# A 7x7 depthwise convolution as matmuls: the halo loads' queue and who empties PSUM

## The chip, the cores and the metric

The kernel runs on one core of one Trainium2 chip. The metric is the device time of one execution in microseconds. A core has five engines that run their own instruction streams: TensorE (PE in the profile, PEld for its weight loads), VectorE (DVE), ScalarE (ACT), GpSimd (POOL) and SyncE (SP). DMAs are issued from SP, ACT or POOL and are carried out by 16 DMA engines. Matmuls write into PSUM, from which DVE and ACT copy to SBUF.

## The reference

Two layers over a tensor x of 384 channels and 192 x 192 pixels, in fp32. Layer 0 is an attention over channels; layer 1 is a depthwise 7x7 convolution. Each takes a group norm of its input and adds its result to it:

```
x = x + L0_conv(groupnorm(x))       # qkv 1x1, 2x2 max pool, 3x3 depthwise, channel attention, gelu, repeat, projection
x = x + L1_conv(groupnorm(x))       # what the change touches

def L1_conv(x, weight):             # weight: (384, 1, 7, 7)
    w_sym = (weight + rot90(weight, 1) + rot90(weight, 2) + rot90(weight, 3)) * 0.25
    return depthwise_conv(x, w_sym, stride=1, pad=3)
```

## The kernel before

The kernel goes through the image four times. It reads x for the statistics of the first norm; computes pooled, depthwise-filtered q, k and v and the products of q and k; mixes v and writes the input of layer 1, channel by channel, into DRAM tiles `sd` and `sh` (L558 to L642); and last does the 7x7 stage (L651 to L853), which the change is in.

**The 7x7 stage** takes 8 channels (CB) in each of 48 steps. A channel's 192 rows are cut into 6 tiles (NT) of 32 rows (TR), and its columns into 4 classes by their remainder modulo 4 (CP). So 4 x 32 = 128 partitions hold one channel's rows by column class, and the free dimension is 6 tiles x 48 columns (NJ) = 288. The 7x7 filter becomes three matmuls per channel that add up in PSUM: two with `main`, the second one column along, and one with `aux`, which holds in partitions 0 to 63 a copy of a part of `main`, shifted by two columns, and in partitions 64 to 93 and 96 to 125 the halo: three rows above and three below each tile, in 10 column classes (NQ). The weight matrices, 128 x 384 per channel, were built earlier and lie in DRAM tile `wt`.

**The loop** (L809) is software-pipelined by hand. In iteration n it traces, in this order: the loads of step n + 2 (`load_w` L675: one DMA of 1536 KB; `load_main` L680: one of 1200 KB for `main`, two of 281.2 KB for the halo in `aux`); on POOL the `borders` of step n + 1 (L741: two corrections at the columns at the edges, the shifted copy into `aux` at L761, two corrections at its edges, and two fills at L770 where the halo lies outside the image); on POOL and SP the `spread` of step n - 1 (L790: two interleaving copies at L794 from `apart` to `res`, then eight stores of 144 KB at L798, the first four after the first copy, the others after the second); and then the matmuls of step n (L825, L830, L836) with their evictions. Between the second and the third pair of channels DVE adds the residual's diagonal to the next step's weights (`middle`, L784).

**Evictions.** A pair of channels, q of 0 to 3, has one PSUM tile `ps` of two banks; four such tiles are in rotation. Each is emptied in four pieces, one for each quarter g of 32 partitions, with both channels at once (32 x 576 elements), multiplied by the channel's 1/std. The pieces go to `apart`, of which two are in rotation.

**Order.** Every instruction of the loop is traced through `keep`, which holds an engine's instructions in the order of the program. Waits between engines are put in by the framework. DMAs of SP and ACT take their completion semaphores in turn from eight, so that a DMA is issued only when the one before on the same semaphore has landed. `main` and the weights have three buffers each, and `aux` is one of three tiles in rotation.

Of the kernel before, what the change touches and what calls it, by code (L numbers as in the profile page):

```python
# [74 lines left out]
def conv_preact_d2(  # L75
# [17 lines left out]
    nc = tc.nc  # L93
# [28 lines left out]
    for kt in range(KT):  # L122
        g = gsel[:, kt, :].rearrange("p (g j) -> p g j", j=GC)
# [527 lines left out]
    with ExitStack() as ex_:  # L651
# [20 lines left out]
        def span(n):  # L672
            return slice(n * CB, (n + 1) * CB)

        def load_w(n):  # L675
            w = wtp.tile([P, CB, 3 * P], F32, name=f"w{n}", tag="w")
            keep(nc.sync.dma_start(w, wt[:, span(n)]))
            return w

        def load_main(n):  # L680
            main = mainp.tile([P, CB, NT, JP], F32, name=f"main{n}", tag="main")
            keep(nc.sync.dma_start(main.rearrange("p c t j -> p c (t j)"), sd[:, span(n)]))
            aux = auxs[n % len(auxs)]
            af = aux.rearrange("p c t j -> p c (t j)")
            for base, h in ((TOP, 0), (BOT, HALO)):
                keep(
                    nc.sync.dma_start(
                        af[base : base + HALO * NQ], sh[h * NQ : (h + HALO) * NQ, span(n)]
                    )
                )  # L690
            return main, aux

        ws = {n: load_w(n) for n in range(2)}
        mains = {n: load_main(n) for n in range(2)}

        mean1, rstd1, _ = group_stats(st.rearrange("p t b n s -> p t (b n) s"), "1")
# [44 lines left out]
        def borders(n):  # L741

            main, aux = mains[n]
            cs = span(n)

            def border(t, lo, hi, j, k, nj):
                part = t[lo:hi, :, :, j : j + nj]
                keep(
                    nc.gpsimd.tensor_tensor(
                        part, part,  # L750
                        mm[lo:hi, cs, k : k + nj].unsqueeze(2).to_broadcast(
                            [hi - lo, CB, NT, nj]
                        ),
                        ALU.add,
                    )
                )

            border(main, 0, P, 0, 0, 1)
            border(main, 0, P, NJ, 1, 2)
            keep(  # L760
                nc.gpsimd.tensor_copy(  # L761
                    aux[0:TOP, :, :, 0:NJ].rearrange("p c t j -> p (c t) j"),
                    main[0:TOP, :, :, 2 : 2 + NJ].rearrange("p c t j -> p (c t) j"),
                )
            )
            border(aux, TOP, ONE, 0, 3, 1)
            border(aux, TOP, ONE, NJ - 1, 4, 1)
            for base, t in ((TOP, 0), (BOT, NT - 1)):
                keep(
                    nc.gpsimd.tensor_copy(  # L770
                        aux[base : base + HALO * NQ, :, t, 0:NJ],
                        mb[base : base + HALO * NQ, cs].unsqueeze(2).to_broadcast(
                            [HALO * NQ, CB, NJ]
                        ),
                    )
                )

        def middle(n):

            for i in range(0, CB, 4):  # L780
                c = n * CB + i
                mid = ws[n][:, i : i + 4, CENTRE : CENTRE + P]
                keep(
                    nc.vector.scalar_tensor_tensor(  # L784
                        mid, eye.unsqueeze(1).to_broadcast([P, 4, P]), stdb[:, c : c + 1], mid,
                        ALU.mult, ALU.add,
                    )
                )

        def spread(n, apart):  # L790

            res = outp.tile([P, 2, NT * NJ, CP], F32, name=f"res{n}", tag="res")
            for k in range(2):
                keep(nc.gpsimd.tensor_copy(res[:, k], apart[:, :, k].rearrange("p e n -> p n e")))  # L794
            for k in range(2):
                for q in range(CP):
                    keep(
                        nc.sync.dma_start(  # L798
                            out[n * CB + 2 * q + k].rearrange("(t r) w -> r t w", t=NT),
                            res[q * TR : (q + 1) * TR, k].rearrange(  # L800
                                "p (t j) e -> p t (j e)", t=NT
                            ),
                        )
                    )
# [4 lines left out]
        for n in range(steps):  # L809
            if n + 2 < steps:  # L810
                ws[n + 2] = load_w(n + 2)
                mains[n + 2] = load_main(n + 2)
            if n + 1 < steps:
                borders(n + 1)
            if last is not None:
                spread(n - 1, last)
            w, (main, aux) = ws.pop(n), mains.pop(n)
            apart = outp.tile([P, CP, 2, NT * NJ], F32, name=f"apart{n}", tag="apart")
            for q in range(CP):
                ps = pc.tile([P, 2, 512], F32, name=f"pc{n}_{q}", tag="pc")  # L820
                for k in range(2):
                    i = 2 * q + k
                    acc = ps[:, k, 0 : NT * NJ]
                    keep(
                        nc.tensor.matmul(  # L825
                            acc, w[:, i, 0:P], main[:, i, :, 0:NJ], start=True, stop=False
                        )
                    )
                    keep(
                        nc.tensor.matmul(  # L830
                            acc, w[:, i, P : 2 * P], main[:, i, :, 1 : 1 + NJ],
                            start=False, stop=False,
                        )
                    )
                    keep(
                        nc.tensor.matmul(  # L836
                            acc, w[0:KLAST, i, 2 * P :], aux[0:KLAST, i, :, 0:NJ],
                            start=False, stop=True,
                        )
                    )  # L840
                c = n * CB + 2 * q
                for g in range(CP):
                    src = ps[g * TR : (g + 1) * TR, :, 0 : NT * NJ]
                    dst = apart[q * TR : (q + 1) * TR, CP - 1 - g]
                    scale = rb[g * TR : (g + 1) * TR, c : c + 1]
                    if g % 2:
                        keep(nc.scalar.mul(dst, src, scale))  # L847
                    else:
                        keep(nc.vector.tensor_scalar_mul(dst, src, scale))  # L849
                if q == 1 and n + 1 < steps:  # L850
                    middle(n + 1)
            last = apart
# [57 lines left out]
```

## Time and profile before

Three runs took 3204.36, 3206.84 and 3207.24 us: the median is 3206.84 us.

| what | value |
|---|---|
| the profiled execution | 3205.75 us |
| its span | 3204.1 us |
| PE busy | 2698.8 us (84%) |
| DVE busy | 2466.5 us (77%) |
| ACT busy | 740.1 us (23%) |
| POOL busy | 804.1 us (25%) |
| mean granted TensorE clock | 0.949 |
| DMA, mean over the span | 180 GB/s |
| loads of the 7x7 stage's weights, L677 | 48 issues, from 2487.4 to 3163.1 us |

In the profile a line such as L849 is a line of the kernel. A busy time is the time in which an engine executed; loads and stores are not in it. A wait is an engine's idle time, put down to the event that ended it. "SPq" and "ACTq" are the sequencers, which issue the DMAs of SP and ACT; the time beside an issue is that of issuing, not of the transfer. The DMA share is the mean busy share of the 16 DMA engines, and GB/s is what they moved.

### The profile page before, as it was taken

The page shows a single profiled execution, that of the slowest core. Times are in us where ns is not written, and L with a number is a line of the kernel's source. Part 1 is how long each engine was busy: PE and PEld are TensorE (multiplying, and loading weights), DVE is VectorE, ACT ScalarE, POOL GpSimd, SP SyncE. Part 2 cuts the span into 40 slices and gives each one's busy share as a digit, 9 for nine tenths or more (in the row PEclk, how much of TensorE's full clock was granted, in tenths as well). Part 3 has the DMA queues.
Part 4 walks back from the last instruction along what each step waited for, and adds up shares of the span by engine and source line. Part 5 has one row for each costly group of instructions (what it writes and reads, how often), then busy time and mean ns, then how long its engine had stood idle before and what let it go on. Part 6 is the DMA issues. An engine that isn't in the chain of part 4 may idle for free. (4 is left out here: it accounts for less than half of the span.)

```text
span 3204.1 us, 25358 instructions
## 1 busy us (share of the span) xinstructions
PE 2698.8 (84%) x8243; PEld 1529.8 (48%) x8243; DVE 2466.5 (77%) x3993; ACT 740.1 (23%) x1545; POOL 804.1 (25%) x959
## 2 busy tenths in 40 slices
PE   0079999999999999999999998355784599898997
PEld 0044444444444444444444444234562476666665
DVE  7957878888888877778888888775999676656665
ACT  0001222222222222222222222011211144434443
POOL 0044343100000000000000001143122366667666
PEclk9999999999999999999999999577997699999998
DMA  9946666311111111111111000399999699999998
GB/s 376 372 138 229 208 215 223 103 40 61 46 37 37 37 37 37 37 38 39 38 37 53 27 8 14 124 392 391 362 364 314 213 325 333 320 317 332 328 322 272
DMA packets 205379, 576.50 MB, mean 180 GB/s; under 512 B 18672, under 2 KB 131680, under 8 KB 190080
## 3 DMA queue, kind: packets, MB, share of 16 engines
q1 hardware_dynamic: 156496, 395.82, 35.7%
q0 software_dynamic: 43776, 175.52, 15.8%
q10 hardware_dynamic: 4976, 3.56, 0.3%
q8 instruction: 66, 1.08, 0.1%
q14 instruction: 65, 0.53, 0.1%
HBM read 341.56 MB, written 233.10 MB: 179 GB/s over the span
## 5 line engine op out<-in xcount | busy, mean ns | idle before, releaser
L348 PE MATMUL pq<-xq,wq 128*128 128x512 f32 x3402 | 1474.0, 592 | 0.0
L348 PEld LDWEIGHTS pq<-xq,wq 128*128 128x128 f32 x3402 | 640.0, 190 | 773.5 <-issue 719.2
L384 DVE SCALAR_TENSOR_TENSOR qk<-pad,wd,qk 128x384 f32<-128x384 f32 x1152 | 690.6, 617 | 52.9 <-ACT pad L363 40.7
L355 DVE TENSOR_REDUCE t<-pq 128x128 f32<-128x512 f32 x648 | 444.9, 687 | 253.4 <-PE pq L348 253.4
L849 DVE TENSOR_SCALAR apart<-pc,rb 32x576 f32<-32x576 f32 x384 | 311.1, 810 | 245.3 <-ACT apart L847 156.7
L438 POOL DMA_DIRECT2D vd<-vb x72 | 57.7, 802 | 1350.4 <-DVE vb L384 1350.4
L847 ACT ACTIVATE apart<-pc,rb 32x576 f32<-32x576 f32 x384 | 281.7, 734 | 446.1 <-DVE apart L849 362.3
L384 DVE SCALAR_TENSOR_TENSOR vb<-pad,wd,vb 128x384 f32<-128x384 f32 x576 | 337.5, 614 | 20.5 <-ACT pad L363 18.5
L836 PE MATMUL pc<-aux,w 127*128 127x288 f32 x768 | 262.1, 423 | 42.4 <-POOL aux L770 42.3
L363 ACT ACTIVATE pad<-t,bq 128x96 f32<-128x96 f32 x207 | 77.9, 376 | 931.6 <-DVE t L355 931.6
L608 DVE TENSOR_TENSOR sx<-xr,y 128x576 f32<-128x576 f32 x192 | 222.3, 1212 | 74.9 <-ACT y L597 39.1
L825 PE MATMUL pc<-main,w 128*128 128x288 f32 x768 | 260.3, 421 | 19.5 <-DVE w L784 9.6
L830 PE MATMUL pc<-main,w 128*128 128x288 f32 x768 | 258.6, 419 | 0.0
L348 PE MATMUL pq<-xs,wq 128*128 128x512 f32 x486 | 215.3, 603 | 0.0
L794 POOL COPY res<-apart 128x1152 f32<-128x1152 f32 x96 | 210.0, 2220 | 18.6 <-ACT apart L847 8.2
L577 PE MATMUL po<-v,attnT 128*128 128x288 f32 x448 | 126.6, 438 | 89.3 <-DMA v<-vd 84.0
L836 PEld LDWEIGHTS pc<-aux,w 127*128 127x128 f32 x768 | 150.1, 198 | 96.2 <-POOL aux L770 54.1
L190 PE MATMUL gs<-mv,gsel 128*128 128x1 f32 x36 | 8.5, 353 | 220.9 <-DVE mv L180 218.0
L825 PEld LDWEIGHTS pc<-main,w 128*128 128x128 f32 x768 | 149.2, 196 | 70.4 <-POOL res L794 11.7
L590 PE MATMUL pr<-gl,wp 128*128 128x288 f32 x576 | 154.4, 424 | 32.1 <-ACT y L597 32.0
L830 PEld LDWEIGHTS pc<-main,w 128*128 128x128 f32 x768 | 149.9, 195 | 45.1
L615 DVE BATCH_NORM_STATS2 st<-sx 128x6 f32<-128x288 f32 x384 | 149.8, 474 | 0.2
(128 smaller groups left out, 2044.9 us busy)
## 6 DMA issues: line engine op xcount, KB each, us to landing
w<-wt SPq DMA_DIRECT2D x48, 1536.0 KB, 6.8
sd<-sx POOLq DMA_DIRECT2D x96, 600.0 KB, 10.2
main<-sd SPq DMA_DIRECT2D x48, 1200.0 KB, 11.7
xs<-in_x_dram SPq DMA_DIRECT2D x24, 2304.0 KB, 11.6
xr<-in_x_dram SPq DMA_DIRECT2D x48, 1152.0 KB, 27.1
out_dram<-res SPq DMA_DIRECT2D x384, 144.0 KB, 7.2
xq<-in_x_dram SPq DMA_DIRECT2D x21, 2304.0 KB, 8.2
wt<-g POOLq DMA_DIRECT2D x24, 1152.0 KB, 6.7
```

Of the source, the lines that this page charges most:

```text
L348: nc.tensor.matmul(ps, wq[:, kt, ct * P : (ct + 1) * P], rows[:, kt, :, g * 64 : (g + 1) * 64], start=(kt == 0), stop=(kt == KT - 1),)
L355: nc.vector.tensor_reduce(t[:, :, g * 32 : (g + 1) * 32], ps.rearrange("p (h a w b) -> p h w a b", h=PR, a=2, b=2), AX.XY, ALU.max,)
L384: nc.vector.scalar_tensor_tensor(dst, win, w, dst, ALU.mult, ALU.add)
L590: nc.tensor.matmul(ps[:, h, 0:H], wp[:, ct, ot * P : (ot + 1) * P], gl[:, ct, h * H : (h + 1) * H], start=(ct == 0), stop=(ct == KT - 1),)
L608: nc.vector.tensor_tensor(sx[:, v, :, :, dj : dj + NJ], xq[:, :, :, :, e], y[:, :, :, e // 2].unsqueeze(1).to_broadcast([P, RB, NT, NJ]), ...
L615: nc.vector.bn_stats(st[:, ot, b, v * RB + a, :], sx[:, v, a, :, dj : dj + NJ])
L794: keep(nc.gpsimd.tensor_copy(res[:, k], apart[:, :, k].rearrange("p e n -> p n e")))
L825: nc.tensor.matmul(acc, w[:, i, 0:P], main[:, i, :, 0:NJ], start=True, stop=False)
L830: nc.tensor.matmul(acc, w[:, i, P : 2 * P], main[:, i, :, 1 : 1 + NJ], start=False, stop=False,)
L836: nc.tensor.matmul(acc, w[0:KLAST, i, 2 * P :], aux[0:KLAST, i, :, 0:NJ], start=False, stop=True,)
L847: keep(nc.scalar.mul(dst, src, scale))
L849: keep(nc.vector.tensor_scalar_mul(dst, src, scale))
```

## The change

The two halo loads of `load_main` are issued from ACT instead of SP; their place in the traced program is the same, between `main`'s load and the borders. And the engine that takes a piece of PSUM is chosen by the pair q, no longer by the quarter g: pairs 0 and 2 go to DVE whole, pairs 1 and 3 to ACT whole.

```
@@ -684,7 +684,7 @@
             af = aux.rearrange("p c t j -> p c (t j)")
             for base, h in ((TOP, 0), (BOT, HALO)):
                 keep(
-                    nc.sync.dma_start(
+                    nc.scalar.dma_start(
                         af[base : base + HALO * NQ], sh[h * NQ : (h + HALO) * NQ, span(n)]
                     )
                 )
@@ -843,7 +843,7 @@
                     src = ps[g * TR : (g + 1) * TR, :, 0 : NT * NJ]
                     dst = apart[q * TR : (q + 1) * TR, CP - 1 - g]
                     scale = rb[g * TR : (g + 1) * TR, c : c + 1]
-                    if g % 2:
+                    if q % 2:
                         keep(nc.scalar.mul(dst, src, scale))
                     else:
                         keep(nc.vector.tensor_scalar_mul(dst, src, scale))
```

## The prediction

> **What bounds the kernel now.** The edit is inside the loop of L809, so only the end of the span matters. I read the slices of the page first (from slice 31 the DMA is at 9 of 10), then the stage in windows, then SP's queue, then the waits. From 2540 to 3163 us the DMA share is 0.99, PE is busy 567 of 623 us at a granted clock of 0.96, DVE 392, POOL 405, ACT 267. One step, in windows of 1.04 us (times; busy of PE, PEld, DVE, ACT, POOL; clock; DMA share; GB/s):
>
> ```profile
> 2874.62:2875.66 1.04, 1.04 (x2) 0.76 (x3) 0.00 (x0) 0.36 (x1) 1.04 (x1) 0.50 1.05 437
> 2877.74:2878.78 1.04, 1.04 (x4) 0.75 (x3) 0.00 (x0) 0.00 (x0) 1.04 (x1) 0.50 1.02 425
> 2880.86:2881.90 1.04, 1.04 (x6) 0.77 (x5) 0.47 (x1) 0.53 (x1) 0.00 (x0) 1.00 1.10 210
> 2881.90:2882.94 1.04, 1.04 (x6) 0.82 (x5) 0.37 (x1) 0.20 (x1) 0.00 (x0) 1.00 0.85 163
> 2882.94:2883.98 1.04, 1.04 (x6) 0.82 (x5) 0.43 (x1) 0.57 (x1) 0.00 (x0) 1.00 0.86 236
> 2883.98:2885.02 1.04, 1.04 (x6) 0.80 (x5) 0.81 (x1) 0.16 (x1) 0.50 (x2) 1.00 0.98 326
> ```
>
> The engines of the DMA are occupied all along, but for some 3 us they move 163 to 236 GB/s instead of 425. SP's queue says what is under way then:
>
> ```profile
> 2871.52 0.36 SPq L677 DMA_DIRECT2D w<-wt  x1
> 2871.92 0.43 SPq L682 DMA_DIRECT2D main<-sd  x1
> 2872.40 0.91 SPq L687 DMA_DIRECT2D aux<-sh  x2
> 2876.75 9.02 SPq L798 DMA_DIRECT2D out_dram<-res  x8
> 2885.93 0.34 SPq L677 DMA_DIRECT2D w<-wt  x1
> ```
>
> One queue in that order: weights, main, two halo loads, eight stores. The slow stretch is where the halo's turn comes. The waits of SP's own queue, 2600 to 3180 us (total, times, longest):
>
> ```profile
> SPq L798 <- DMA main<-sd: 151.5, 42, 5.8
> SPq L798 <- POOL res L794: 132.0, 47, 4.3
> SPq L798 <- DMA aux<-sh: 49.4, 76, 1.7
> SPq L798 <- DMA w<-wt: 11.0, 15, 1.3
> SPq L677 <- PE pc L836: 0.4, 1, 0.4
> ```
>
> Stores wait for loads: a DMA is issued once the one eight issues before it has landed, so the last four stores wait for weights, main and both halos, and the next step's weights follow within 0.5 us. PE holds L677 only once. So a step lasts as long as its loads take to land: 44 steps from 2548.5 to 3163.1 us, 13.97 us each. Last, the waits of the engines:
>
> ```profile
> ACT apart L847 <- DVE apart L849: 325.2, 255, 4.8
> POOL main L749 <- DMA main<-sd: 168.2, 38, 7.3
> DVE apart L849 <- ACT apart L847: 137.1, 168, 0.9
> PE pc L836 <- POOL aux L770: 42.3, 24, 3.1
> ```
>
> The largest wait, ACT's for DVE, is the hand-over inside one PSUM tile (DVE, ACT, DVE, ACT). It is not the bound: DVE's cycle for one pair is 0.81 + 0.80 of waiting + 0.81 = 2.4 us, four pairs and the two L784 (1.1 us each) 11.9 us, under 13.97; and PE waits for POOL's borders, which wait for main.
>
> **The change, step by step.**
>
> (a) Bytes of a step, from the page's list of issues (KB of 1024): weights 1.57 MB, main 1.23, halos 0.58, stores 1.18, together 4.56 MB (13.97 us at 326 GB/s; the stage shows 322). Weights and main at 425 take 6.6 us, stores at 326 take 3.6, so 3.8 us are left for 0.58 MB of halo: 150 GB/s, as the slow windows show. In 3.8 us there are two parts: 1.35 us that these bytes would take at 425, and 2.4 us in which engines and whatever shares their path are held up.
>
> (b) The halo goes to a second queue. In the built program each aux load on ACT follows the second and the fourth store of an earlier step, so it can run beside the last stores and the weights, not behind main. Upper bound of the gain: the whole 2.4 us, but PE needs 48 matmuls per step, started every 0.243 us at full clock (pairs 0.485 us apart): 11.7 us, at the granted 0.96 12.2. So at most 13.97 - 12.2 = 1.8 us. Lower bound, a loss: issue intervals of L677 reach 15.5 us in the slow steps of this trace, 1.5 us above the mean. The nearest row for two queues at once is the stage before (2062 to 2480): POOL's and SP's queue together move 365 GB/s at a DMA share of mostly 9, so a second queue costs nothing by itself there. Main's time to landing in this stage is 8.7 / 11.5 / 13.4 us (least, median, most), and the fast steps of this trace, with main near 10, last 12.9 to 13.1. I take a step of 13.2, a gain of 0.8 us: between no gain and the 1.8, and near those fast steps, since the halo's bytes remain and only their company changes. 44 x 0.8 = 35 us.
>
> The Trainium skill ("DMA: Bandwidth & Descriptors", Issuing engines are not separate DMA queues) speaks against it: all queues run on the same 16 engines, and a second issuer saves only issue time. The share of 1.0 agrees; by that rule this term is 0. Another page ("SBUF — State Buffer", Door 1: the DMA port swizzle) has partitions 64 to 127, where the halo lies, reach 8 of 16 ports, about 218 GB/s; the 163 to 236 GB/s agree. By an estimate from it the odd ports take half of weights and main plus the halo, 1.98 MB, in 9.1 us, against 10.4 now: a gain of up to 1.3.
>
> (c) SP is rid of two issues (0.44 us each by L687's row). They follow main's, so they are not between a landing and the next weights: 0. But main is now the last load to land. Main landed 0.3 us before the first halo and about 1 us before the second (stores 6 to 8, released by them, start 2884.40 to 2885.45). POOL's borders hang on main: a shift of about +1 us, once, as the loop of loads does not wait for POOL.
>
> (d) ACT gets the two issues, 0.9 us per step, beside 8 x 0.734 = 5.9 us of evictions: 6.8 of 13.2 us. More matters where they stand: behind the last eviction of a step, ahead of q = 1 of the next, waiting for stores 2 and 4. These follow main in SP's ring and land some 0.9 and 1.8 us after it (eight stores in 3.6 us). So ACT is held where DVE now starts, until about 2.5 us after main's landing, then evicts q = 1 and q = 3 in 2 x 2.94 us. In this step:
>
> ```profile
> 2878.86 0.81 DVE L849 TENSOR_SCALAR apart<-pc,rb 32x576 f32<-32x576 f32 x1 [4.65 <-POOL res L794]
> 2879.76 0.73 ACT L847 ACTIVATE apart<-pc,rb 32x576 f32<-32x576 f32 x1 [4.78 <-DVE apart L849]
> 2884.52 0.66 POOL L749 TENSOR_TENSOR main<-main,mm 128x48 f32<-128x48 f32 x2 [5.70 <-DMA main<-sd]
> 2889.88 0.51 PE L836 MATMUL pc<-aux,w 127*128 127x288 f32 x1 [0.55 <-POOL aux L770]
> ```
>
> Main lands at 2884.4, ACT would begin near 2887 and free q = 1's tile near 2890. PE wants it after the first pair of the next step: four of its 12 matmuls are done at 2889.88, so at 2889.88 + 8 x 0.243 = 2891.8: 1.8 us to spare. POOL reads the result one step later. Cost 0; once the cover is gone, each us of hold is a us of PE's wait, of which DMA's slack takes the first.
>
> (e) Evictions by one engine: the counts stay (8 ACT, 8 DVE per step), the hand-overs go. DVE's wait of 137 us and ACT's of 325 shrink, worth 0, since late next is POOL's main, as now. At the end of the kernel the last tile takes ACT 4 x 0.734 = 2.9 us against 0.81 + 0.73 + 0.81 + 0.73 + gaps = 3.2: -0.3. The start (2489 to 2548) hangs on the group statistics, not on halos: 0.
>
> Sum: -35 + 1 - 0.3 = -34 us. The profiled execution took 3205.75 us (span 3204.1), so 3171.5; it lies 1.1 under the median 3206.84, so 3173.
>
> **Rivals.**
>
> R1, hidden anyway: the halo costs the engines the same wherever it queues; step 13.97, time 3207. For it: share 0.99 already. Against it: the same engines move 425.
>
> R2, the whole slow stretch is absorbed and PE becomes the bound: 12.2 us, 44 x 1.8 = 79, time 3128. For it: PE waits for borders only 42 us. Against: it leaves no room for the wait on L770.
>
> R3, the slower side: the halo, now among the weights of every engine, holds weights and main up as it now holds main's tail. Place: L677's and L682's landing. It decides when they together land more than 0.8 us later than the halo's absence from the tail saves; at two thirds of the 1.5 us of slow steps, +1.0 x 44 = 44, time 3251. Against it: the stage before with two queues.
>
> R4, ACT's hold passes the 1.8 us to spare, and PE then starves by more than the 1.8 us that it has over DMA: with 1.0 us of that per step net, less what (b) gains at the ring, some +0.8 x 44 = 35, time 3242. Place: L825 on the tiles of q = 1 and 3.
>
> The edit does what it says: in the built program both aux loads are on ACT, and pairs are whole.
>
> **How the numbers follow.** Forecast 0.48, R2 0.13, R1 0.13, R3 0.16, R4 0.10. The measurement tells 0.2%, 6.4 us, from no change. Faster 0.61, same 0.13, slower 0.26. The forecast's own range, 0.3 to 1.4 us per step, is 3146 to 3194. To 8 in 10 it takes in R2 and R1 and the near half of R4 and R3: 3125 to 3242.
>
> **What would show it.** (b): L677 issued every 13.2 us; the windows at 160 to 240 GB/s gone, main landing within 10.5 us. (c): POOL still waits for main, SP's stores no longer for aux. (d): ACT's largest wait is for stores, PE's rows on pc show no wait for ACT. (e): ACT and DVE no longer wait for each other. Wrong if w and main land later than 6.8 and 11.7 us by more than the step gains, or if PE waits for L847.

## The result, and the profile after

The changed kernel took 3326.03 us (median of four runs, 3324.99 to 3328.42) against 3206.66 us for the kernel before (now four runs): a ratio of 1.0375, 95% interval 1.0357 to 1.0393. It is 119 us slower; the forecast was 3173 us, 34 us faster. The profiled execution has a span of 3326.2 us and a mean granted clock of 0.935 (0.949 before).

From the fifth weight load of the 7x7 stage to the last (w<-wt, L677: 2566.0 to 3283.6 us, 43 steps) a step takes 16.69 us; the same measure of the kernel before gives 14.01. 43 x 2.68 = 115 us, so that nearly the whole loss is in the steady loop.

The stage in one window (columns: times; busy of PE, PEld, DVE, ACT and POOL; clock; DMA share; GB/s):

```profile
2552.00:3283.00 731.00, 602.34 (x2160) 440.31 (x2158) 359.81 (x450) 264.66 (x361) 377.95 (x389) 0.89 0.84 275
```

The DMA engines, the bound before at a share of 0.99 and 322 GB/s, now stand idle for a sixth of the stage. PE is busy for 602 of 731 us, at a lower clock. Nothing is saturated: something waits. SP's queue over a step and a half (start, us, what; the time beside a row covers the waits between its first and last issue):

```profile
2873.46 0.40 SPq L677 DMA_DIRECT2D w<-wt  x1
2873.90 0.49 SPq L682 DMA_DIRECT2D main<-sd  x1
2874.49 13.73 SPq L798 DMA_DIRECT2D out_dram<-res  x8
2888.34 0.40 SPq L677 DMA_DIRECT2D w<-wt  x1
```

The two issues of halo loads are gone from it, as the edit says. But the eight stores, which took 9.0 us to issue before, now take 13.7. What SP waited for, 2600 to 3280 us (total, times, longest):

```profile
SPq L798 <- DMA aux<-sh: 338.4, 70, 11.6
SPq L798 <- DMA w<-wt: 124.5, 41, 4.2
SPq L798 <- POOL res L794: 16.4, 17, 2.9
```

SP's wait for halos was 49.4 us when it issued them itself; now that ACT issues them it is 338.4 us. The engines' waits in the same stretch:

```profile
ACT apart L847 <- PE pc L836: 412.7, 79, 14.1
POOL main L749 <- DMA main<-sd: 306.5, 39, 12.3
DVE apart L849 <- POOL res L794: 292.0, 41, 9.6
PE pc L836 <- POOL aux L770: 77.2, 36, 3.0
```

ACT waits for PE, POOL for main, DVE for POOL: a ring in which everyone is late. ACT's timeline shows where the halo's issue stands in it:

```profile
2875.38 2.98 ACT L847 ACTIVATE apart<-pc,rb 32x576 f32<-32x576 f32 x4 [4.12 <-PE pc L836]
2881.08 0.73 ACT L847 ACTIVATE apart<-pc,rb 32x576 f32<-32x576 f32 x1 [2.72 <-PE pc L836]
2881.09 1.99 ACTq L687 DMA_DIRECT2D aux<-sh  x2
```

The four evictions at 2875.38 are pair 1, the one at 2881.08 is the first of pair 3. The halo loads are issued 0.01 us after that, and PE's last matmul of the step had ended at 2881.04. In ACT's program the halo stands behind an eviction that can't start before PE is done with the whole step. It could not go out earlier in any case: with three `aux` tiles, the halo of step n + 3 is written into the tile that PE reads until the end of step n. The chain that ended last, in order of time, from one weight load to the next but one (start, us, what):

```profile
2873.46 0.40 SPq L677
2873.90 9.36 DMA main<-sd
...
2883.66 0.40 POOL main L749
...
2884.11 2.11 POOL aux L761
...
2887.44 0.52 POOL aux L770
...
2888.00 1.33 PE pc L836 x2
...
2899.90 0.50 PE pc L836 x2
2900.42 0.33 ACT apart L847
2900.79 4.35 DMA aux<-sh
2905.16 0.32 SPq L798
2905.48 0.05 issue
2905.59 0.38 SPq L677
```

This is the new bound. Weights and main of a step are issued; main lands 9.8 us after the weights' issue; the borders take POOL 4.7 us; PE works for 12.4 us; then ACT's first eviction of pair 3 starts, and with it the halo of three steps later is issued; it lands after 4.7 us; a store on SP goes out at once, and 0.45 us after the landing SP issues the weights of the step after the next. Together 32.1 us for two steps, 16.1 per step in this turn (16.7 on the mean). Two steps of work that used to overlap now stand partly one behind the other. Over the whole stage (2600 to 3280 us) the chain goes the same way: 50% of it is PE, 19% main, 18% the halo.

Why a store on SP waits for a halo that ACT issued: the two engines draw their completion semaphores from one set (in the trace, numbers 100 and 102 to 108), in the order of the whole built program. There the halo of step 24 is followed on its two semaphores by stores 6 and 8 of step 19. In the trace these two stores were issued at 2886.93 and 2887.82 us, and the two halos had landed by 2886.9 and 2887.8. On SP these stores stand ahead of the weights of step 23 (2888.34 us). So the weights of a step now wait for the halo of the step after it; the trace has the same order in 40 of the last 41 steps. Before the change they waited for the halo of the step before it: the weights of step 27 (2885.93 us) stood behind stores 7 and 8 of step 23, and those waited for the halo of step 26, which SP had issued right after the weights of step 26.

While SP waits, the DMA engines run dry (same columns as the first window):

```profile
2885.50:2886.50 1.00, 0.26 (x1) 0.00 (x0) 0.00 (x0) 0.00 (x0) 0.94 (x2) 0.50 0.57 115
2886.50:2887.50 1.00, 0.00 (x0) 0.00 (x0) 0.00 (x0) 0.00 (x0) 0.90 (x4) 0.50 0.16 38
2887.50:2888.50 1.00, 0.50 (x1) 0.50 (x2) 0.00 (x0) 0.00 (x0) 0.94 (x2) 0.50 0.60 129
```

The stretch at 163 to 236 GB/s with busy DMA engines gave way to one at 38 to 129 GB/s with idle ones. The transfers themselves are not slower: weights land 6.4 us after their issue (6.8 before), main 11.0 (11.7), the halo 4.4 (11.9).

### The profile page after: what moved, and what is told of

Same layout as the page of the kernel before. It is cut to its first block, busy times and chain, and to the rows that moved or that the text cites. A ratio compares the mean times of both kernels' runs of the same rounds, so it can differ in the third digit from the quotient of the medians.

```text
span 3326.2 us, 25418 instructions
## 1 busy us (share of the span) xinstructions
PE 2742.5 (82%) x8243; PEld 1550.2 (47%) x8243; DVE 2440.9 (73%) x3993; ACT 741.4 (22%) x1545; POOL 782.6 (24%) x959
## 5 line engine op out<-in xcount | busy, mean ns | idle before, releaser
L836 PE MATMUL pc<-aux,w 127*128 127x288 f32 x768 | 275.1, 441 | 80.3 <-POOL aux L770 80.2
L825 PE MATMUL pc<-main,w 128*128 128x288 f32 x768 | 277.3, 445 | 56.1 <-POOL main L749 51.6
L608 DVE TENSOR_TENSOR sx<-xr,y 128x576 f32<-128x576 f32 x192 | 231.3, 1307 | 77.7 <-ACT y L597 36.2
L830 PE MATMUL pc<-main,w 128*128 128x288 f32 x768 | 273.0, 440 | 0.0
L794 POOL COPY res<-apart 128x1152 f32<-128x1152 f32 x96 | 207.4, 2191 | 16.5 <-ACT apart L847 13.7
L825 PEld LDWEIGHTS pc<-main,w 128*128 128x128 f32 x768 | 156.5, 207 | 112.1 <-POOL main L749 61.3
L830 PEld LDWEIGHTS pc<-main,w 128*128 128x128 f32 x768 | 159.3, 207 | 50.5
L615 DVE BATCH_NORM_STATS2 st<-sx 128x6 f32<-128x288 f32 x384 | 159.0, 570 | 0.2
```

The source lines that it names most:

```text
L608: nc.vector.tensor_tensor(sx[:, v, :, :, dj : dj + NJ], xq[:, :, :, :, e], y[:, :, :, e // 2].unsqueeze(1).to_broadcast([P, RB, NT, NJ]), ...
L615: nc.vector.bn_stats(st[:, ot, b, v * RB + a, :], sx[:, v, a, :, dj : dj + NJ])
L825: nc.tensor.matmul(acc, w[:, i, 0:P], main[:, i, :, 0:NJ], start=True, stop=False)
L830: nc.tensor.matmul(acc, w[:, i, P : 2 * P], main[:, i, :, 1 : 1 + NJ], start=False, stop=False,)
L836: nc.tensor.matmul(acc, w[0:KLAST, i, 2 * P :], aux[0:KLAST, i, :, 0:NJ], start=False, stop=True,)
```

## The experiments

Every ratio is to the kernel before, run on the same chip in the same group of runs (3218.4 to 3220.9 us there). Expected times that start from 3207 or 3326 us (e1, e2, e13) lie some 12 us low for these groups.

**The queue alone.**

```
-                    nc.sync.dma_start(
+                    nc.scalar.dma_start(
                         af[base : base + HALO * NQ], sh[...]
```

> The halo loads on ACT as in the changed kernel, but the evictions as before (quarters in turn). Theory 1, the held halo: on ACT the halo of step k+3 stands behind the last eviction of step k, which waits for the end of PE's step k, and stores and loads on SP that share its completion semaphores wait for its landing, so that SP's next loads hang on PE. Then the loss of 119 us comes with the queue alone: 3300 to 3400 us (later still than the changed kernel by up to 2.5 us per step, since ACT's last piece here is the fourth quarter of the last pair). Theory 2, a second queue slows the transfers themselves: 3326 us, and weights and main land later than 6.8 and 11.7 us after their issue. Theory 3, whole pairs leave PSUM later and PE starves: 3207 us.

3329.25 us, ratio 1.0344 (1.0316 to 1.0372). SP's waits, 2600 to 3280 us:

```profile
SPq L682 <- DMA aux<-sh: 318.6, 38, 11.3
SPq L798 <- DMA main<-sd: 85.1, 37, 4.6
```

The whole loss comes with the queue. With the evictions by quarters it is mostly main's issue, L682, that stands behind the halo, and only now and then a store (29.7 us). The sum of the wait is about the same.

**The evictions alone.**

```
-                    if g % 2:
+                    if q % 2:
```

> Evictions by whole pairs, the halo loads on SP as before. Theory 1 and theory 2: no loss, 3200 to 3210 us, since DMA sets the step; the hand-over waits between ACT and DVE go all the same. Theory 3: the whole loss, some 3326 us.

3216.21 us, ratio 0.9994 (0.9983 to 1.0005): no change, though 6 us above the range in us. The engines' waits, 2600 to 3180 us:

```profile
ACT apart L847 <- PE pc L836: 330.0, 83, 10.0
DVE apart L849 <- POOL res L794: 213.2, 40, 8.6
DVE apart L849 <- ACT apart L847: 5.4, 2, 2.7
```

The hand-overs are gone (ACT's wait for DVE from 325 us to none shown, DVE's for ACT from 137 to 5) and nothing is gained: both engines wait for PE and POOL instead.

**The halo on POOL's queue, evictions by pairs (e3) and by quarters (e8).**

```
-                    nc.sync.dma_start(
+                    nc.gpsimd.dma_start(
                         af[base : base + HALO * NQ], sh[...]
```

> Whole pairs, and the halo loads on POOL's queue, a second queue too, but with completion semaphores that SP's loads and stores do not share. Theory 1: the loss goes; 3170 to 3235 us, the lower end if the halo in a queue of its own disturbs main's tail less, the upper if POOL's two issues (0.8 us each by the issues of L438) cost PE time. Theory 2: the second queue slows the transfers here too, some 3326 us. Theory 3: 3326 us.

> The halo on POOL's queue, the evictions by quarters as before. If the gain of 43 us is the queue's alone: 3170 to 3185 us. If whole pairs have a share in it now that DMA is faster (the evictions' cycle of 11.9 us per step is near 12.8): 3185 to 3215 us.

e3: 3175.24 us, ratio 0.9863 (0.9848 to 0.9877). e8: 3179.61 us, 0.9876 (0.9855 to 0.9897). The stage of e3 in one window:

```profile
2540.00:3125.00 585.00, 553.28 (x2216) 420.14 (x2216) 416.72 (x471) 266.78 (x364) 469.81 (x505) 0.98 1.00 350
```

And SP's waits in e3, 2600 to 3100 us:

```profile
SPq L798 <- POOL res L794: 164.8, 43, 5.2
SPq L798 <- DMA main<-sd: 15.8, 17, 4.0
```

SP waits for no halo, the DMA share is 1.00, the same bytes move at 350 instead of 322 GB/s, and a step takes 12.8 us. POOL's queue does gain what the forecast hoped for from a second queue. Its halos share no semaphores with SP's stores: the trace has them on 111 to 118 and SP's DMAs on 100 and 102 to 108. Measured from PE's end the halo is not earlier than on ACT. Pair 3 of step 21 and the halo of step 24 in e3:

```profile
2825.02 2.96 ACT L847 ACTIVATE apart<-pc,rb 32x576 f32<-32x576 f32 x4 [2.73 <-PE pc L836]
2828.79 1.01 POOL L687 DMA_DIRECT2D aux<-sh  x2
```

It goes out 3.8 us after the first eviction of that pair (the median over the steps is 5.6), where on ACT it was 0.01 us. So on POOL's queue a halo that comes after PE's end costs nothing by itself; what matters is who waits for it.

**Is it the halo's place on ACT?** In e4 ACT takes pairs 0 and 1, so that the halo stands behind pair 1 and not pair 3, and `aux` has a fourth tile. In e5 `apart` has a third tile too; in e6 the changed kernel has only that third tile, and in e7 the kernel of e3 has it.

```
-        for i in range(3):
+        for i in range(4):
             t = wide.tile([P, CB, NT, JP], F32, name=f"aux{i}")
...
-                    if q % 2:
+                    if q < CP // 2:
```

```
+        apartp = ex_.enter_context(tc.tile_pool(name="apartp", bufs=3))
...
-            apart = outp.tile([P, CP, 2, NT * NJ], F32, name=f"apart{n}", tag="apart")
+            apart = apartp.tile([P, CP, 2, NT * NJ], F32, name=f"apart{n}", tag="apart")
```

> The changed kernel with four aux tiles in place of three, and ACT taking pairs 0 and 1 and DVE 2 and 3. So neither the tile nor ACT's place holds the halo until PE's step ends: ACT comes to it after the second pair, 24 matmuls or 5.8 us earlier at full clock. Theory 1: the loop of two steps, 35 us, becomes about 29, a step of 14 to 14.7 us in place of 16.6: 3210 to 3245 us. Theory 2: 3326 us. Theory 3: 3326 us or more, as two pairs in turn wait for one engine.

> The run with four aux tiles and ACT on pairs 0 and 1, and a third apart tile, so that ACT's evictions no longer wait for POOL's copies either. Theory 1, now: what holds the halo on ACT is whatever the eviction ahead of it waits for (PE's end in the changed kernel, POOL's copy to res in the run before); with both gone it is PE's second pair, and the loop of two steps is halo 6 + stores and weights' issue 2 + main 11 + borders 4.6 + two pairs 5.8 = 29.4 us, a step of 14.7: 3225 to 3245 us. Theory 4, the halo's place on ACT is no matter and only the extra tiles or the second queue are: as the run before, 3290 us.

> The changed kernel with a third apart tile and nothing else, so that DVE's 292 us of waiting for POOL's copies go. Theory 1: no gain, 3315 to 3330 us, since the halo waits for the end of PE's step as before. Theory 4, POOL's hold on apart is what slows the changed kernel: back to 3215 to 3240 us.

> The halo on POOL's queue, whole pairs, and a third apart tile: is the kernel at 3175 us still held by evictions that wait for POOL (139 us of DVE's)? If DMA and PE set its step of 12.8 us (DMA share 1.00, PE 553 of 585 us), no gain: 3165 to 3180 us; if the evictions do, down to PE's 12.0 us per step, 3140 us.

e4: 3291.97 us, ratio 1.0228 (1.0211 to 1.0246). e5: 3289.92 us, 1.0219 (1.0204 to 1.0235). e6: 3345.85 us, 1.0394 (1.0374 to 1.0415). e7: 3176.55 us, 0.9865 (0.9841 to 0.9889). e4 and e5 take away a good third of the loss and miss what was expected of them by 45 us or more; e6 ends 16 us above its range. ACT's waits in e4 and then in e5 (whose lines stand one further down), 2600 to 3280 us:

```profile
ACT apart L847 <- POOL res L794: 400.2, 43, 13.6
```

```profile
ACT apart L848 <- PE pc L837: 224.7, 39, 12.9
ACT apart L848 <- POOL res L795: 173.5, 14, 15.7
```

SP still waits 359.8 us (e4) and 352.3 us (e5) for halos. In e4 the evictions that now stand ahead of the halo wait for POOL to empty `apart`; with a third `apart` they wait for PE in most steps, and for POOL still in 14. Whatever holds ACT delays the halo, and through the halo SP. A better place on ACT shortens the loop and doesn't open it. The third `apart` tile by itself gains nothing, with the loop (e6) or without it (e7).

**Are the shared semaphores the link?** With four stores of two channels each, a step issues eight DMAs from SP and ACT, as many as there are semaphores. Then each halo load follows the halo load of the step before, and no store follows a halo; in the traces of e9 and e15 the halos are on 108 and 102, from step 9 on with nothing else between them. The edit went into the changed kernel (e9), the kernel before (e10) and e3 (e11).

```
-            for k in range(2):
-                for q in range(CP):
-                    keep(nc.sync.dma_start(out[n * CB + 2 * q + k]..., res[q * TR : (q + 1) * TR, k]...))
+            for q in range(CP):
+                c = n * CB + 2 * q
+                keep(nc.sync.dma_start(out[c : c + 2]..., res[q * TR : (q + 1) * TR]...))
```

> The changed kernel with the eight stores of a step issued as four (both channels of a pair in one, the same bytes). ACT's place for the halo is as in the changed kernel. But a step now has eight DMAs on SP and ACT, as many as there are completion semaphores, so that in the built program each halo load shares its semaphore with the next step's halo load alone, and no store or load of SP waits for a halo. Theory 1 in its present form, it takes both ACT's place and the shared semaphore: the loss goes, 3165 to 3215 us. Theory 5, the late halo itself holds POOL's borders and PE: 3290 us or more still.

> The control: the kernel before with four stores in place of eight, the halo on SP. Here too SP's stores no longer wait for the step's own loads. If the DMA engines set the step (share 0.99 before): 3195 to 3215 us. If SP's waits did: faster, 3150 to 3190 us, and then the run beside it has to be read against this one.

> The halo on POOL's queue, whole pairs, and four stores in place of eight. The kernel at 3175 us has a DMA share of 1.00 and PE busy 553 of 585 us: if both are at their end, 3165 to 3180 us; if the remaining waits of SP for POOL and main cost time, 3140 to 3165 us.

e9: 3285.81 us, ratio 1.0204 (1.0189 to 1.0219), a miss by 70 us and more. e10: 3244.52 us, 1.0073 (1.0058 to 1.0088), slower where no change or a gain was expected. e11: 3259.13 us, 1.0119 (1.0093 to 1.0145), 79 us above the range expected. SP's waits in e9, 2600 to 3180 us:

```profile
SPq L798 <- POOL res L794: 282.1, 37, 8.3
...
SPq L798 <- DMA aux<-sh: 9.7, 2, 5.9
```

The wait for halos is all but gone, as meant, but the edit has a price of its own: each store now needs both copies of `res`, and the kernel before loses 24 us by it, e3 84. Against its control e10, e9 is 41 us slower, where the changed kernel is 119 us slower than its own. So some 78 us went with the shared semaphores, and 41 were left. The 78 is a difference between kernels with different limits, since SP now waits for POOL's copies most; a part of the loop's cost may be hidden behind that wait. In these kernels weights land late, in e9 later than in e10 (the lists of DMA issues; the last column is the median us to landing):

```profile
w<-wt SPq DMA_DIRECT2D x48, 1536.0 KB, 13.2
```

```profile
w<-wt SPq DMA_DIRECT2D x48, 1536.0 KB, 10.0
```

**Only the order of the loads changed.** The kernel before with all loads on SP, in the order halo, main, weights:

```
-                ws[n + 2] = load_w(n + 2)
                 mains[n + 2] = load_main(n + 2)
+                ws[n + 2] = load_w(n + 2)
```

and within `load_main` the two halo loads ahead of main's.

> The kernel before, all on SP's queue, but with a step's loads in the order halo, main, weights, so that the halo follows the stores and not main. It asks where the 43 us of POOL's queue come from. If from the halo's company (its bytes no longer run against the tail of main): 3165 to 3195 us. If from its being in a queue of its own, which the engines serve in turn with SP's: 3200 to 3215 us.

3192.43 us, ratio 0.9911 (0.9896 to 0.9927), as expected. About 28 us of what e8 gains need no second queue: it is enough that the halo follows stores and not main. The order also changes what SP's last stores wait for (in e12, 2600 to 3130 us: weights 119.9 us, main 76.0, halos 22.0), so the run doesn't show how much of the 28 us comes from which transfers run side by side and how much from these waits.

**Waits or bytes?** The last four runs keep every DMA and every wait and cut each halo load to one channel of eight, so that the output lacks most of the halo.

```
-                        af[base : base + HALO * NQ], sh[h * NQ : (h + HALO) * NQ, span(n)]
+                        af[base : base + HALO * NQ, 0:1], sh[h * NQ : (h + HALO) * NQ, n * CB : n * CB + 1]
```

> The changed kernel with each halo load cut to one channel of eight (36 KB instead of 281 KB; the other seven channels keep what the tile was filled with, so the output lacks most of the halo). Number, order and places of the DMAs stay. Theory L (loop of waits: PE's end, ACT's eviction of q = 3, the halo's issue, its landing, SP's stores 6 and 8, the next weights): only the landing gets shorter, from 5.8 to some 2.5 us, so that the loop of two steps drops from 35.1 to 31.8 us and the step by 1.6 us: 3326 - 44 x 1.6 = 3255, between 3220 and 3290, with SP still waiting for aux by more than 150 us in total. Theory B (the halo's bytes beside weights and main cost the time): seven eighths of the cost goes with the bytes, the time falls to within 30 us of the kernel before with the same cut.

> The control: the kernel before with the same cut of the halo loads (one channel of eight, all DMAs on SyncE's queue). The halo takes 3.8 us of the step's 13.97 by the sums made so far, and seven eighths of that would go; PE's 48 matmuls at 12.2 us are the next bound. Both theories: 12.2 to 12.8 us per step, 3128 to 3155.

> The changed kernel with four stores of two channels per step, and the halo cut to one channel of eight. Here no store shares a completion semaphore with a halo. What was left over with the full halo, 3285.8 against 3244.5 us of the kernel before with four stores, is either the halo's bytes beside weights and main (then this kernel is within 10 us of the kernel before with four stores and the same cut), or a hold of the halo or of ScalarE's queue that bytes do not set (then it stays 25 us or more above it).

> The control: the kernel before with four stores of two channels per step, and the halo cut to one channel of eight. Four stores cost 24 us with the full halo, at a DMA share of 0.99; with less to move, 3130 to 3190.

| the four with short halos | us | ratio to before | per step, us |
|---|---|---|---|
| e13, changed, eight stores | 3296.39 | 1.0242 (1.0215 to 1.0269) | 15.84 |
| e14, before, eight stores | 3146.63 | 0.9781 (0.9763 to 0.9799) | 12.21 |
| e15, changed, four stores | 3203.93 | 0.9956 (0.9940 to 0.9972) | 13.42 |
| e16, before, four stores | 3197.02 | 0.9935 (0.9919 to 0.9952) | 13.18 |

With the halo's bytes nearly gone the changed kernel loses 150 us to its control, more than the 119 with full halos: the loss is waits, not bytes. SP's waits in e13, 2600 to 3250 us:

```profile
SPq L798 <- DMA aux<-sh: 292.5, 41, 10.3
```

And in e14, 2600 to 3120 us:

```profile
SPq L798 <- POOL res L794: 135.0, 50, 5.6
```

A piece of e13's chain that ended last:

```profile
2873.46 0.50 PE pc L836 x2
2874.00 2.62 DMA aux<-sh
```

The loop starts in the same way, with PE's end and then the halo, and SP waits for halos nearly as long; only the halo's own part shrank, from 4.4 to 2.6 us in these turns (medians of all: 4.4 and 1.8). It was expected to save 1.6 us per step and saved 0.85 (16.69 to 15.84), so that e13 ends 6 us above its range; e16 ends 7 us above its own. e15 has the halo at the same place on ACT, behind PE's end, but shares no semaphore with stores: it is 7 us slower than its control. So with short halos the place alone costs next to nothing, and the place with shared semaphores costs 150 (in e15 and e16, too, four stores set a limit of their own: e16 is 50 us slower than e14).

The 41 us between e9 and e10 drop to 7 with short halos, so 34 of them belong to the halo's bytes on ACT's queue in the kernel with four stores. That it is weights and main that the halo holds up there is likely from the 13.2 against 10.0 us, and not shown: on POOL's queue in e11 weights land after 10.4 us, and that kernel is also 15 us slower than e10. This rest stays open.

## Why the prediction was wrong, point by point

(a) held as a sum of bytes, but its 150 GB/s are not the halo's rate alone: the slow windows (2880.86 to 2883.98 us) lie before main's landing at 2884.4, so main's tail is in them, and they don't test the rate of eight ports either. Short halos gave a size: e14 needs 12.21 us per step, 1.8 less than before, for seven eighths of the halo less. More could not show, as other limits are next. PE's 12.2 us are near (busy 541 of 560 us), but the chain of e14, 2563 to 3090 us, lies mostly on the evictions, with their hand-overs (the view ends the line where it breaks off):

```profile
by line: DVE apart L849 40.2%; ACT apart L847 18.3%; DVE w L784 14.1%; PE pc L825 7.5%; PE pc L836 7.4%; PE pc L830 7.4%; issue 2.6%; DMA main<-sd 1.9%; POOL aux L761 0.4%; POOL aux L749 0.1%; ACTq L847 0.1%; POOL main L749 0.1%; SPq L677 0
```

That is the prediction's cycle of 11.9 us, rightly called no bound at 13.97, but as near as PE's once the step is short.

(b) is the step that failed, in one half. Its gain was about right in size: with the halo on another queue that shares nothing with SP's stores, e8 gains 40 us and e3 44 (0.0124 and 0.0137 of 3207), where 35 was forecast. The slow windows get rarer and don't vanish: of the windows of 1 us in the stage, 90 of 600 move under 240 GB/s at a DMA share of 0.8 or more before, 36 of 560 in e3, 22 of 560 in e8. Its reading of the semaphores was half done. The prediction looked up which DMAs the halo follows ("each aux load on ACT follows the second and the fourth store of an earlier step") and not which DMAs follow the halo. Those are stores 6 and 8 on SP, ahead of the next weights. The wait of SP for a halo that can't start before PE's end was put at nothing; it measured 338 us. So the two bounds, a gain of 1.8 and a loss of 1.5 us per step, left out the case that happened, a loss of 2.7. The lower bound was also misread: the longest interval between two weight loads of the loop before is 16.2 us (2560.8 to 2577.1), not 15.5, and the steps in which the trace shows main's landing after 9.6 to 10.4 us last 12.9 to 13.95, not 12.9 to 13.1.

(c) put SP's two issues at nothing, which no run tests apart. Its mark, that SP's stores no longer wait for aux, came out the other way: 49 us became 338.

(d) priced the wrong wait. It placed the halo's issue rightly behind an eviction of ACT, took the stores ahead of it as what it waits for, and asked who waits behind it on ACT. In the trace the halo waits for no store; it goes out with the first eviction of pair 3, when PE ends its step. ACT's largest wait is for PE (412.7 us), not for stores. Who waits for the halo's landing on another engine's queue was not asked, and there the cost arose. After the fact the sum can be made from parts of one turn of the changed kernel: main 9.8, borders 4.7, PE 12.4, halo 4.7 and 0.45 for SP make 32.1 us for two steps.

(e) was right: with the halo on SP, e2 gives 0.9994.

The rivals. R3 had the sign but not the mechanism: weights and main land no later than before. R4 had ACT's hold, but PE starving on PSUM tiles; PE's waits, 2600 to 3280 us, are for POOL's borders (77.2 us at `aux`, 50.3 at `main`) and none is for ACT's evictions, and the starving engine was SP. R1 and R2 are out: the halo's place in the order is worth 28 us on SP's own queue (e12), and a step of 12.2 us was reached only with short halos (e14).

The Trainium skill ("DMA: Bandwidth & Descriptors", Issuing engines are not separate DMA queues) says that DMAs of several issuing engines run on the same 16 DMA engines and that issuing from several saves only the time of issuing. Measured, the halo on POOL's queue raises the stage from 322 to 350 GB/s and the kernel gains 1.2 to 1.4%. e12 reconciles most of it: 0.9% comes from the order of the loads on one queue alone, and a second queue changes the order too.

## What to carry to other kernels

When a DMA moves to another engine's queue, ask two things: what stands ahead of it in that engine's program, and who is issued next on its completion semaphore, on every queue that draws from the same set. If what stands ahead waits for the compute of a step, and what stands behind is ahead of a later step's loads, the pipeline has been closed into a loop, and its length can be estimated from rows of the trace. A late start alone is no loss: in e3 the halo starts later still. Where only the order of transfers needs to change, change it on one queue (e12), or use a queue with semaphores of its own (e3).

## What was not expected of the hardware

- The same 0.58 MB of halo per step costs different times by its place in the order: all on SP's queue, behind main, a step takes 14.0 us; ahead of main and behind the stores, 13.2 us (e12).
- Fewer and larger stores were slower: four of 288 KB instead of eight of 144 KB cost 24 us on SP alone and 84 us beside the halo on POOL's queue. SP's wait for POOL's copies (254 to 287 us in e9, e10 and e11, against 132 before) is the likely reason; it was not tried apart.
- In the changed kernel PE stood idle from 2881.04 to 2883.76 us, and the clock granted was 0.79 in the window from 2883.50 to 2884.50 us and 0.50 in the following ones, with PE at work in part of them. The Trainium skill ("TensorE: Matmul & The Clock Gate", Part 1: The HAM clock gate) speaks of an idle window of about 3.4 us before the clock halves; here a gap of 2.7 us was enough. The loop so lengthens itself: from 2888.00 us on PE had 44 of its 48 matmuls left and took 12.4 us, where 44 x 0.243 = 10.7 would do.
